# Hybrid block on one core: loads to the front, ten maximum steps into the loop, TensorE's order written out

## The chip, the cores and the metric

The kernel runs on one core of a Trainium2 chip. The metric is the device time of one execution in microseconds; the time before is the median of three runs. A profile of one further execution gives the duration of every instruction, what each engine waited for, and what the DMA queues moved.

## The reference

The kernel computes four residual stages over 2 x 2048 tokens of 256 features, all in 32-bit floats: a grouped-query attention, a feed-forward rotation, a linear attention and the feed-forward rotation again. Only the first stage is touched here:

```python
x = x + attn_a(layernorm(x))
# attn_a(x):                      B=2, N=2048, 16 query heads in 4 groups over 4 key heads, head size 16
q = x @ Wq + bq;  k = x @ Wk + bk;  v = x @ Wv + bv
scores = einsum('bghnd,bhsd->bghns', q, k)
attn   = softmax(scores / 4, axis=-1)        # over all 2048 keys of the batch
out    = einsum('bghns,bhsd->bghnd', attn, v)
return out @ Wo + bo
```

## The kernel before

**Blocks and units.** Tokens are handled in eight blocks of 512 (`NB = 8`; `BPB = 4` blocks make a batch). A unit is one block of queries with one of the four groups, so there are 32 units. For each unit the softmax needs the largest score of every query, and only then the exponentials. The kernel computes the scores twice. `largest()` makes them with queries on partitions (`s`, L378), and VectorE reduces each 128 x 512 tile to its maximum (`mx`, L382): 64 such maximum steps per unit. At the end of a unit `turn_maxima` transposes the negated maxima (`pm`, L398), ScalarE copies them (`mr`), and four DMAs on SP put them into `mrows` (`a_m`, L405). The main loop makes the scores again with keys on partitions (`p`, L633), adds the maxima with a second matmul (the shift, L637), takes the exponential on ScalarE (`e`, L641) and weighs the values (`av`, L620). It has 16 loop steps per unit, each with four scores, four shifts, four exponentials and four weighings. In each loop step four maximum steps of a later unit are mixed in with `next(ahead)`. So the maxima run ahead of the loop by a lead: `LEAD = 80` maximum steps are issued before the loop begins, that is the whole of unit 0 and sixteen of unit 1.

**The prologue** is everything before the loop. For block j, `arrive(j)` loads the tokens (`xs`, L255), `look(j)` computes mean and variance on VectorE and the scale on POOL, `spread(j)` normalizes into `z`, `features(j)` transposes on TensorE (`tr`) and copies out (`zb`), `keys(j)` multiplies by the key and value weights (`pk`), splits the keys into a high and a low half (`kh`, `kl`), stores the halves to DRAM (`dk`, L244) and fetches them in the layout that the scores need (`a_kP`, L249). `asked(j, m)` projects queries (`pq`, L337), `project(u)` stores and fetches a unit's queries (`dq`, `qP`), and `values(j)` transposes the values (`pv`). Blocks 0 to 3 are written out by hand; the rest is the generator `pieces()`, one piece after every third lead step. `biases` multiplies selection rows with the bias columns (`a_pbias`, `a_pbq`); their copies `bkv` and `bq` are used by `keys` and `asked`. `rows()` loads the output weights (`a_wo`, eight DMAs, and `a_bo`) and makes the output bias row.

**Queues and order.** SP issues its DMAs in order: one that waits for computed data holds those behind it. Before the change the loads of blocks 0 to 3 are at the front of SP's order, block 4 is behind the stores and fetches of block 1's keys (L543), and blocks 5 to 7, two constants and the output weights are behind unit 1's queries (L560 to L567). ACT's queue carries the weights at the start.

The framework may move instructions of an engine; `in_order` ties them to the program's order. Before the change, all five engines are tied at the loop's start, for what was issued up to there:

```python
            in_order(begin, (engines.PE, engines.DVE, engines.Activation, engines.Pool, engines.SP))
```

In the built program the first loop steps' scores on TensorE stand among the last lead steps: after the fourth score of the first loop step, for instance, four lead steps follow before its first shift. The maximum steps of unit 0 take their banks from two pools (`psp` with four, `pss` with three); later units use the three of `pss` alone. The loop's `p` tiles use the four of `psp`.

Of the kernel before, what the change touches and what calls it, by code (L numbers as in the profile page):

```python
# [16 lines left out]
P = 128  # L17
# [50 lines left out]
def tile_hybrid(ctx: ExitStack, tc: tile.TileContext, x: bass.AP, consts: bass.AP, wa_d: bass.AP, wf_d: bass.AP, wb_d: bass.AP, out: bass.AP):  # L68
# [84 lines left out]
    def attention_a():  # L153
        with ExitStack() as st:
# [41 lines left out]
            def biases(raw, at, bqr, sel):  # L196


                pb = psp.tile([P, BLK], F32, tag="p", name="a_pbias")
                rows, bv = sel[:, 0:64], sel[0:1, 64:P]  # L200
                compact(rows, ident, nc.scalar.copy)
                compact(bv, raw[0:1, at["bv"][0] : at["bv"][1]], nc.scalar.copy)
                mm(pb[0:64, 0:1], rows, raw[:, at["bk"][0] : at["bk"][1]], start=True, stop=True)
                mm(pb[64:P, 0:1], bv, ones[0:1, 0:1], start=True, stop=True)
                pq = psp.tile([P, BLK], F32, tag="p", name="a_pbq")
                for e in range(2):
                    mm(pq[64 * e : 64 * e + 64, 0:2], rows, bqr[:, e::2], start=True, stop=True)
                nc.vector.tensor_copy(bkv, pb[:, 0:1])
                nc.vector.tensor_copy(bq, pq[:, 0:2])
# [52 lines left out]
            def look(j):  # L262

                st = own.tile([P, 4, 6], F32, tag="ln_st", name=f"st_a{j}", bufs=4)
                mv = own.tile([P, 4, 2], F32, tag="ln_mv", name=f"mv_a{j}", bufs=4)
                rs, nb = (own.tile([P, 4], F32, tag=f"ln_{t}", name=f"{t}_a{j}", bufs=4) for t in ("rs", "nb"))
                for t in range(4):
                    if t == 3:
                        yield
                    nc.vector.bn_stats(st[:, t, :], xs[:, 4 * j + t, :])  # L270
                for t in range(4):
                    nc.vector.bn_aggr(mv[:, t, :], st[:, t, :])
                nc.vector.tensor_scalar(rs, mv[:, :, 1], EPS, None, ALU.add)
                nc.gpsimd.tensor_tensor(rs, rs, const("mhalf"), ALU.pow)
                nc.vector.tensor_scalar(nb, mv[:, :, 0], -1.0, None, ALU.mult)
                nc.gpsimd.tensor_tensor(nb, nb, rs, ALU.mult)
                looks[j] = mv, rs, nb
                yield

            normal, planes, kvs = {}, {}, {}  # L280

# [206 lines left out]
                        nc.vector.tensor_tensor(xs[:, 4 * j + t, :], xs[:, 4 * j + t, :], po[:, 0:D], ALU.add)  # L488
                        yield

            LEAD, WARM = 64 + 16, 4
            ahead = largest()
            begin = len(nc.cur_bb.bb.instructions)
            loads = ExitStack()
# [12 lines left out]
            arrive(1)  # L507
            nc.scalar.dma_start(wqb, wa_d[:, slice(*_WA["wq"])])
            nc.scalar.dma_start(bqr, wa_d[:, slice(*_WA["bq"])])
            arrive(2)  # L510
            arrive(3)

            nc.vector.memset(still, 0.0)
            idle = psp.tile([P, BLK], F32, tag="p", name="idle")
# [5 lines left out]
            for n, first in (("wk", 0), ("wv", 64)):  # L520
                for c in range(2):
                    lo = at[n][0] + c * P
                    compact(wkv[:, c, first : first + 64], raw[:, lo : lo + P], nc.scalar.copy)
            list(look(0))
            biases(raw, at, bqr, sel)
            one, two, three = look(1), look(2), look(3)
            next(one)
            spread(0, ld, 2)
            next(one)
            features(0, ld, 1)  # L530
            compact(wq.rearrange("p c d -> p (c d)"), wqb, nc.gpsimd.tensor_copy)
            spread(1, ld, 2)
            keys(0, ld)()
            features(1, ld, 0)
            list(two)
            asked(0, 0)
            first = project(0, nc.gpsimd)
            spread(2, ld, 2)
            list(three)
            first()  # L540
            second = keys(1, ld)
            second()
            arrive(BPB)  # L543
            values(0)
            features(2, ld, 1)
            spread(3, ld, 2)
# [10 lines left out]
            next(ahead)  # L557
            next(ahead)
            project(1)()
            nc.sync.dma_start(small[:, P : _CONST["ones"][0]], consts[:, P : _CONST["ones"][0]])  # L560
            nc.sync.dma_start(
                small[:, _CONST["ones"][1] : _CONST["mhalf"][0]], consts[:, _CONST["ones"][1] : _CONST["mhalf"][0]]
            )
            for j in range(BPB + 1, NB):
                arrive(j)
            more = rows()
            next(more)  # L567

            def memsets():
                for t in mrows[0] + mrows[1]:  # L570
                    nc.gpsimd.memset(t.bitcast(F32), 0.0)
# [4 lines left out]
            def pieces():  # L576

                memsets()
                list(look(4))
                values(3)  # L580
                for j in range(1, BPB):
                    for m in range(2):
                        asked(j, m)
                        yield
                        if (j, m) == (2, 0):
                            spread(4, ld, 0)
                next(more)
                for j in range(BPB, NB):
                    features(j, ld, 0)
                    if j + 1 < NB:  # L590
                        list(look(j + 1))
                    yield
                    keys(j, ld)()
                    if j + 1 < NB:
                        spread(j + 1, ld, 0)
                    yield
                    asked(j, 0)
                    yield
                    asked(j, 1)
                    values(j)  # L600
                    if j == BPB:
                        next(more)
                    yield

            rest = pieces()
            for n in range(4, LEAD):
                next(ahead)
                if n % 3 == 1:
                    next(rest, None)
                if n == 67:  # L610
                    for f in later:
                        f()
                    later.clear()
            in_order(begin, (engines.PE, engines.DVE, engines.Activation, engines.Pool, engines.SP))

            av, last, done, norms = None, None, iter(()), iter(())

# [5 lines left out]
                    )  # L623

            for u, kb in ((u, kb) for u in range(len(units)) for kb in range(KB)):
                qP, mrow = queries[u], mrows[u % 2]
                k0 = units[u][0] // BPB * N + kb * P
                t, es = [], []

                def score(r):  # L630
                    row = slice(64 * (r % 2), 64 * (r % 2) + 64)
                    t.append(psp.tile([P, BLK], F32, tag="p", name=f"p{u}_{kb}_{r}"))
                    mm(t[r], kP[r // 2][row, k0 : k0 + P], qP[r // 2][row, :], start=True, stop=False)  # L633

                def shift(r):
                    row = slice(64 * (r % 2), 64 * (r % 2) + 64)
                    mm(t[r], pick[row, :], mrow[r // 2][row, :], start=False, stop=True)  # L637

                def exp(r):
                    es.append(sb.tile([P, BLK], F32, tag="e", name=f"e{u}_{kb}_{r}", bufs=8))  # L640
                    nc.scalar.activation(es[r], t[r], AF.Exp, scale=1.0 / HD**0.5)  # L641

                ready = list(later)
                later.clear()

                next(ahead, None)
                next(ahead, None)
                score(0)
                score(1)
                shift(0)  # L650
                shift(1)
                exp(0)
                exp(1)
                if kb == 1:
                    next(done, None)
                score(2)
                next(ahead, None)
                score(3)
                shift(2)
                next(ahead, None)  # L660
                shift(3)
                exp(2)
                exp(3)
                for f in ready:
                    f()
                if last is not None:
                    if last[1] == 0:
                        av = pav.tile([P, BLK], F32, tag="av", name=f"av{last[0]}")
                    weigh(*last)
                    if last[1] == KB - 1:  # L670
                        done = finish(last[0], av)
                last = u, kb, es
                if kb > 1:
                    next(done, None)
                    next(norms, None)
                if u % G == 1 and kb == 1 and G < u < 4 * G:
                    norms = norm(u // G - 1)
                if kb == 4 and u + 2 < len(units):
                    project(u + 2)()
                if rest is not None and next(rest, "end") == "end":  # L680
                    rest = None
                    loads.close()
                    late = later_pools["late"] = ctx.enter_context(tc.tile_pool(name="late", bufs=1, side="right"))
                    for n, (name, of) in enumerate((("wf", wf_d), ("wb", wb_d))):
                        weights[name] = late.tile([P, of.shape[1]], F32, name=name)
                        nc.sync.dma_start(weights[name], of)
                    for name in ("w4", "b3"):
                        at = slice(*_WF[name])
                        nc.sync.dma_start(weights["wf"][64:P, at], wf_d[0:64, at])
# [804 lines left out]
```

## Time and profile before

| | us |
|---|---|
| median of three runs | 2184.47 |
| lowest, highest | 2184.06, 2188.18 |
| the profiled execution, its own time | 2182.7 |
| its span, first to last instruction | 2180.8 |
| first maximum (`s`) on TensorE | 28.83 |
| unit 0's maxima turned (`pm`) | 101.04 |
| first shift of the loop (L637) | 105.58 |
| weighing of the fourth loop step begins | 124.26 |

A row of the timeline gives the start, the duration, engine, line, operation, output and inputs, the shape and a count; in brackets stands the idle time of the engine just before, and what ended it. A row of the windows gives, for a stretch of time, its length and then the busy time of PE, PEld (weight loads), DVE (VectorE), ACT (ScalarE) and POOL (GpSimd), each with its count, then the granted share of TensorE's clock, the mean busy share of the DMA engines, and GB/s. A row of the groups gives the count, the busy time, the mean duration in ns, and the idle time before with what ended it.

### The profile page before, as it was taken

The numbers are of one execution on the slowest core, as the hardware profiler recorded it, in microseconds if no ns is written. First come the engines' busy times: TensorE is split into PE (matmuls) and PEld (weight loads), VectorE is DVE, ScalarE is ACT, GpSimd is POOL, SyncE is SP. The second block draws the span as 40 slices with busy tenths as digits, with TensorE's granted clock in tenths as the row PEclk, the third lists the DMA queues.
The fourth block names the chain that finished last, engine by engine and source line by source line (L and its number), as shares of the span: only waits on it lengthen the run. The fifth ranks groups of instructions, "written<-read, shape, count | busy, mean of one in ns | idle before, by whom it ended". The sixth has DMA issues, their size and how long they took to land.

```text
span 2180.8 us, 38972 instructions
## 1 busy us (share of the span) xinstructions
PE 2136.0 (98%) x14346; PEld 1028.5 (47%) x14346; DVE 1725.7 (79%) x3319; ACT 1434.0 (66%) x2780; POOL 348.6 (16%) x318
## 2 busy tenths in 40 slices
PE   8899999999999999999999999999999999999998
PEld 3344444444444444444444444444444567676434
DVE  6789998998999899899899899987144688886435
ACT  3367777777776777777677777777864445554442
POOL 3100000000001000000000000000145345541450
PEclk9999999999999999999999999999999999999999
DMA  6410110101101011010110101100100000000002
GB/s 184 135 58 14 41 36 16 46 12 45 36 16 45 10 48 36 16 39 17 48 35 17 36 19 48 36 16 7 51 1 1 1 1 2 1 2 1 1 0 78
DMA packets 53552, 68.21 MB, mean 31 GB/s; under 512 B 18800, under 2 KB 27888, under 8 KB 53104
## 3 DMA queue, kind: packets, MB, share of 16 engines
q1 hardware_dynamic: 52448, 64.26, 10.6%
q8 instruction: 113, 1.85, 0.3%
q10 hardware_dynamic: 720, 0.92, 0.1%
q14 instruction: 79, 0.65, 0.1%
q0 software_dynamic: 192, 0.52, 0.1%
HBM read 35.26 MB, written 25.69 MB: 28 GB/s over the span
## 4 chain that ended last, share of the span: by engine, by line
PE 86%; DVE 8%; DMA 2%; ACT 1%; SPq 1%; issue 1%; POOL 1%; DVEq 0%; ACTq 0%; POOLq 0%
PE av L620 21%; PE s L378 19%; PE p L633 10%; PE q1f L796 7%; PE p L637 7%; DVE mx L382 5%; PE q2f L806 4%; PE pe L1084 2%; PE po L487 2%; PE bpo L1110 1%; PE pv L954 1%; PE pw L954 1%; PE pq L945 1%; PE q3f L816 1%; PE pk L945 1%; DMA xs<-in_x 1%
## 5 line engine op out<-in xcount | busy, mean ns | idle before, releaser
L382 DVE TENSOR_REDUCE mx<-s 128x1 f32<-128x512 f32 x2048 | 1272.9, 683 | 118.1 <-PE s L378 116.4
L641 ACT ACTIVATE e<-p 128x512 f32<-128x512 f32 x2048 | 1060.7, 605 | 356.9 <-PE p L637 353.3
L378 PE MATMUL s<-a_kP,qP 64*128 64x512 f32 x2048 | 706.7, 470 | 19.5 <-DVE mx L382 17.4
L637 PE MATMUL p<-a_m,a_pick 64*128 64x512 f32 x2048 | 589.5, 416 | 0.0
L378 PEld LDWEIGHTS s<-a_kP,qP 64*128 64x128 f32 x2048 | 283.1, 184 | 578.9 <-DVE mx L382 549.8
L620 PE MATMUL av<-e,a_v 128*32 128x512 f32 x4096 | 550.2, 605 | 0.0
L633 PE MATMUL p<-qP,a_kP 64*128 64x512 f32 x2048 | 529.1, 394 | 2.3 <-ACT e L641 2.3
L633 PEld LDWEIGHTS p<-qP,a_kP 64*128 64x128 f32 x2048 | 286.4, 185 | 62.8 <-ACT e L641 26.9
L637 PEld LDWEIGHTS p<-a_m,a_pick 64*128 64x128 f32 x2048 | 283.9, 184 | 29.4
L481 POOL TENSOR_TENSOR oc<-oc,sums 128x512 f32<-128x512 f32 x16 | 20.8, 1299 | 1232.7 <-DMA sums<-dr 907.1
L796 PE MATMUL q1f<-zq,wf 128*128 128x512 f32 x384 | 175.5, 600 | 0.0
L620 PEld LDWEIGHTS av<-e,a_v 128*32 128x32 f32 x4096 | 81.4, 108 | 128.5 <-issue 119.8
L797 ACT ACTIVATE a1f<-q1f,wf 128x512 f32<-128x512 f32 x96 | 66.0, 688 | 99.6 <-PE q1f L796 96.2
L796 PEld LDWEIGHTS q1f<-zq,wf 128*128 128x128 f32 x384 | 70.6, 190 | 98.0 <-issue 86.3
L806 PE MATMUL q2f<-a1f,wf 128*128 128x512 f32 x192 | 89.6, 610 | 0.0
L1090 DVE TENSOR_TENSOR en<-pe,small 128x512 f32<-128x512 f32 x128 | 79.4, 683 | 12.7 <-PE pe L1084 12.6
L835 DVE TENSOR_SCALAR cf<-cf,f_beta,alphaf 128x512 f32<-128x512 f32 x32 | 33.6, 1050 | 53.7 <-ACT cf L834 53.6
L839 POOL TENSOR_TENSOR tf<-cf,zq 128x512 f32<-128x512 f32 x32 | 55.6, 1737 | 92.0 <-DVE cf L835 91.7
L808 ACT ACTIVATE a2f<-q2f,wf 128x512 f32<-128x512 f32 x48 | 32.7, 687 | 54.9 <-PE q2f L806 54.9
L841 POOL TENSOR_TENSOR zq<-zq,tf 128x512 f32<-128x512 f32 x32 | 56.8, 1775 | 3.1 <-DVE tf L838 0.7
L806 PEld LDWEIGHTS q2f<-a1f,wf 128*128 128x128 f32 x192 | 35.2, 193 | 45.3 <-issue 44.4
L840 DVE TENSOR_TENSOR zq<-zq,tf 128x512 f32<-128x512 f32 x32 | 22.2, 693 | 36.2 <-POOL tf L839 36.0
(207 smaller groups left out, 1674.0 us busy)
## 6 DMA issues: line engine op xcount, KB each, us to landing
qP<-dq SPq DMA_DIRECT2D x64, 256.0 KB
dq<-qh SPq DMA_DIRECT2D x62, 128.0 KB
dq<-ql SPq DMA_DIRECT2D x62, 128.0 KB
a_kP<-dk SPq DMA_DIRECT2D x16, 256.0 KB
oc<-avs SPq DMA_DIRECT2D x128, 32.0 KB
sums<-dr SPq DMA_DIRECT2D x128, 32.0 KB
out<-xs SPq DMA_DIRECT2D x16, 256.0 KB
xs<-in_x SPq DMA_DIRECT2D x7, 512.0 KB
```

What stands on the lines that cost most here:

```text
L378: mm(s, qP[r // 2][row, qi * P : (qi + 1) * P], kP[r // 2][row, k0 + kb * BLK : k0 + (kb + 1) * BLK], start=True, stop=True,)
L382: nc.vector.tensor_reduce(mx[:, qi, r : r + 1, kb], s, AX.X, ALU.max)
L620: mm(av[32 * r : 32 * r + 32, :], vA[:, units[u][0] // BPB * KB + kb, 32 * r : 32 * r + 32], es[r], start=(kb == 0), stop=(kb == KB - 1),)
L633: mm(t[r], kP[r // 2][row, k0 : k0 + P], qP[r // 2][row, :], start=True, stop=False)
L637: mm(t[r], pick[row, :], mrow[r // 2][row, :], start=False, stop=True)
L641: nc.scalar.activation(es[r], t[r], AF.Exp, scale=1.0 / HD**0.5)
L796: mm(q1, w1[:, c, m * P : (m + 1) * P], z[:, c, :], start=(c == 0), stop=(c == 1))
L797: nc.scalar.activation(a1[:, m, :], q1, AF.Gelu, bias=b1[:, m : m + 1])
L806: mm(q2, w2[:, c, :], a1[:, c, :], start=(c == 0), stop=(c == 1))
L839: nc.gpsimd.tensor_tensor(t1, cs, z[:, 0, :], ALU.mult)
L841: nc.gpsimd.tensor_tensor(z[:, 1, :], z[:, 1, :], t1, ALU.subtract)
L1090: nc.vector.tensor_tensor(self.ens[t][w], pes[w].rearrange("p (h n) -> p h n", h=4), const("triu").unsqueeze(1).to_broadcast([P, 4, P]), A ...
```

## The change

- SP's loads of blocks 4 to 7, the two constants and the output weights are issued with the first loads, ahead of every store.
- `look` is no longer a generator. `look(1)` is issued after block 0 is normalized and transposed; before, three quarters of its first part stood ahead of block 0's normalization. Both copies of block 0's transposes are on ACT (one was on VectorE).
- `biases` stops after its two selection copies. Its four products are issued after block 0's transposes.
- The lead is 70 maximum steps. Ten more are taken inside the loop, one in every second of the first twenty loop steps.
- The turning of unit 0's maxima is issued at n = 66, ahead of the last projection of block 7; before, at n = 67, behind it.
- Six warm-up products in place of four.
- TensorE is tied to the program's order from the prologue through the first four loop steps, the other four engines at the loop's start as before.

```diff
                 compact(bv, raw[0:1, at["bv"][0] : at["bv"][1]], nc.scalar.copy)
+                yield
                 mm(pb[0:64, 0:1], rows, raw[:, at["bk"][0] : at["bk"][1]], start=True, stop=True)
...
                 for t in range(4):
-                    if t == 3:
-                        yield
                     nc.vector.bn_stats(st[:, t, :], xs[:, 4 * j + t, :])
...
                 looks[j] = mv, rs, nb
-                yield
...
-            LEAD, WARM = 64 + 16, 4
+            LEAD, MORE, WARM = 64 + 6, 10, 6
...
-            arrive(2)
-            arrive(3)
+            for j in range(2, NB):
+                arrive(j)
+            nc.sync.dma_start(small[:, P : _CONST["ones"][0]], consts[:, P : _CONST["ones"][0]])
+            nc.sync.dma_start(
+                small[:, _CONST["ones"][1] : _CONST["mhalf"][0]], consts[:, _CONST["ones"][1] : _CONST["mhalf"][0]]
+            )
+            more = rows()
+            next(more)
...
-            list(look(0))
-            biases(raw, at, bqr, sel)
-            one, two, three = look(1), look(2), look(3)
-            next(one)
+            look(0)
+            picked = biases(raw, at, bqr, sel)
+            next(picked)
             spread(0, ld, 2)
-            next(one)
-            features(0, ld, 1)
+            features(0, ld, 0)
+            look(1)
+            next(picked, None)
             compact(wq.rearrange("p c d -> p (c d)"), wqb, nc.gpsimd.tensor_copy)
...
             second()
-            arrive(BPB)
             values(0)
...
             project(1)()
-            nc.sync.dma_start(small[:, P : _CONST["ones"][0]], consts[:, P : _CONST["ones"][0]])
...
-            for j in range(BPB + 1, NB):
-                arrive(j)
-            more = rows()
-            next(more)
...
             for n in range(4, LEAD):
                 next(ahead)
-                if n % 3 == 1:
-                    next(rest, None)
-                if n == 67:
+                if n == 66:
                     for f in later:
                         f()
                     later.clear()
-            in_order(begin, (engines.PE, engines.DVE, engines.Activation, engines.Pool, engines.SP))
+                if n % 3 == 1:
+                    next(rest, None)
+            in_order(begin, (engines.DVE, engines.Activation, engines.Pool, engines.SP))
...
             for u, kb in ((u, kb) for u in range(len(units)) for kb in range(KB)):
+                if (u, kb) == (0, 4):
+                    in_order(begin, (engines.PE,))
...
                     next(norms, None)
+                if kb % 2 == 1 and u * KB + kb < 2 * MORE:
+                    next(ahead)
```

More of the change, by code (lines that the diff above doesn't have):

```diff
@@ L534, in attention_a @@
             features(1, ld, 0)
-            list(two)
+            look(2)
             asked(0, 0)
@@ L538, in attention_a @@
             spread(2, ld, 2)
-            list(three)
+            look(3)
             first()
@@ L559, in attention_a @@
             project(1)()
[L560 to L563, printed above, removed]
-            for j in range(BPB + 1, NB):
-                arrive(j)
-            more = rows()
-            next(more)
             def memsets():
@@ L578, in pieces @@
                 memsets()
-                list(look(4))
+                look(4)
                 values(3)
@@ L590, in pieces @@
                     if j + 1 < NB:
-                        list(look(j + 1))
+                        look(j + 1)
                     yield
```

## The prediction

> **What bounds the kernel now.** I read the page first: which engine carries the span.
>
> ```profile
> PE 2136.0 (98%) x14346; PEld 1028.5 (47%) x14346; DVE 1725.7 (79%) x3319; ACT 1434.0 (66%) x2780; POOL 348.6 (16%) x318
> ```
>
> PE is called busy 98% of 2180.8 us, so little is left except where PE is seen idle. Everything that the change moves is issued before about 160 us. After some 560 matmuls (unit 1, step 4 of the loop) the two programs hold the same matmuls in the same order. DVE's last difference is in the same place, and POOL's order is the same throughout. So the question is the prologue, up to the first exponentials at 106 us, and the first twenty loop steps. Next come the waits of PE in the timeline, with the wait on DVE that stands behind each.
>
> ```profile
> 36.95 0.50 PE L378 MATMUL s<-a_kP,qP 64*128 64x512 f32 x2
> 41.16 0.49 PE L378 MATMUL s<-a_kP,qP 64*128 64x512 f32 x1 [3.71 <-DVE mx L382]
> 41.59 3.33 PE L337 MATMUL pq<-zb,a_wq 128*128 128x512 f32 x4
> 44.85 1.01 PE L378 MATMUL s<-a_kP,qP 64*128 64x512 f32 x3
> 45.79 1.98 PE L337 MATMUL pq<-zb,a_wq 128*128 128x512 f32 x4
> ...
> 61.63 0.49 PE L378 MATMUL s<-a_kP,qP 64*128 64x512 f32 x1 [4.01 <-DVE mx L382]
> 62.05 3.32 PE L337 MATMUL pq<-zb,a_wq 128*128 128x512 f32 x4
> ```
>
> ```profile
> 38.56 1.40 DVE L270 BATCH_NORM_STATS2 st_a<-xs 128x6 f32<-128x256 f32 x4 [4.28 <-DMA xs<-in_x]
> ...
> 59.03 1.08 DVE L270 BATCH_NORM_STATS2 st_a<-xs 128x6 f32<-128x256 f32 x3 [3.75 <-DMA xs<-in_x]
> ```
>
> PE names the reduction L382 as its releaser, but DVE itself stood still: `look(4)` and `look(5)` are ahead of the reductions in DVE's order and wait for token blocks. Those blocks come late because SP issues them behind stores that wait for computed keys:
>
> ```profile
> 32.12 0.80 SPq L249 DMA_DIRECT2D a_kP<-dk  x2
> 32.96 0.43 SPq L255 DMA_DIRECT2D xs<-in_x  x1
> ...
> 51.28 0.80 SPq L249 DMA_DIRECT2D qP<-dq  x2
> 52.12 0.43 SPq L560 DMA_DIRECT2D small<-in_const  x1
> 52.60 0.43 SPq L561 DMA_DIRECT2D small<-in_const  x1
> 53.07 1.53 SPq L255 DMA_DIRECT2D xs<-in_x  x3
> ```
>
> The first projection after each stall takes 3.33 and 3.32 us where 1.98 is usual. The windows say why (PEclk is the number after POOL):
>
> ```profile
> 42.10:45.40 3.30, 3.30 (x6) 1.18 (x5) 2.00 (x4) 0.44 (x1) 0.00 (x0) 0.50 0.73 204
> 62.60:65.90 3.30, 3.30 (x7) 1.16 (x5) 2.29 (x5) 0.00 (x0) 1.72 (x3) 0.50 0.43 90
> 103.50:106.90 3.40, 2.77 (x10) 1.22 (x10) 3.40 (x7) 0.90 (x2) 0.00 (x0) 1.00 0.28 60
> 107.00:110.30 3.30, 3.30 (x14) 2.49 (x12) 2.72 (x5) 2.25 (x5) 0.00 (x0) 0.50 1.02 426
> ```
>
> Last, the way into the loop. The first shift (L637, 105.58) waits for the turned maxima `pm`, their copy, and four DMAs that start at 102.28; meanwhile DVE works through twelve bare lead steps:
>
> ```profile
> 101.04 0.60 PE L398 MATMUL pm<-small,mt 128*8 128x128 f32 x4
> 102.10 7.35 DVE L382 TENSOR_REDUCE mx<-s 128x1 f32<-128x512 f32 x12 [2.06 <-PE s L378]
> 105.58 0.39 PE L637 MATMUL p<-a_m,a_pick 64*128 64x512 f32 x1
> ```
>
> One maximum step so costs DVE 7.35/12 = 0.61 us, and PE 0.22 (three between projections, 50.28 to 50.95).
>
> **The change, part by part.**
>
> *Loads first, up to the first maximum (28.83 us before).* SP now issues 21 DMAs before its first key store: 4.78 MB, with ACT's 0.92 MB 5.7 MB in all. The trace moved 316 GB/s from 2.5 to 12 us and 361 from 8 to 11.3, so the last load lands between 18.3 and 20.5. SP is held that long, since its issues wait for earlier landings (the eight `a_wo` issues of 0.3 to 0.45 us took 7.74 us behind three token loads). The first key stores go at about 20 instead of 16.78. From that store to the end of both `a_kP` fetches was 5.2 us, so `qP` is fetched at 25.2. It went at 26.31 before, held by `dq` (POOL's stores of the first queries, landed 26.17). `dq` itself comes 1 to 2 us earlier. The first scaling no longer stands behind `look(1)`'s wait for block 1 (9.80), and the biases' products, whose `bqr` landed at 9.0, stand behind the first transposes. Moving block 0's first copy to ACT adds about 0.5 us to that chain. From fetch to first maximum was 2.5 us: 27.7. Bounds: -2.5 (`dq` alone decides) and +2 (the loads at 250 GB/s); I take **-0.8**. Two more warm-up products are four passes of 0.43, ending near 8.4: they cost nothing, because PE's next work waits for block 0 until past 9.
>
> *The token stalls go.* 3.71 + 4.01 us, and the slow windows behind them: 1.35 + 0.28 and 1.34 + 0.30 on the projection and the three maxima. Together 11.0. What is late next? Two looks, 2.0 us of DVE each, ran inside the stalls and now fall among the reductions, where DVE has 0.7 us spare per piece (48.24, 50.82). `look(6)`, in that position already, holds PE for 0.81 (71.66), so I give back 0.8. POOL's 22.3 us wait for `a_bo` goes too, with nothing behind it that PE needed. Keys don't take over: SP's later fetches had finished at 32.9, 40.7 and 46.3 and now follow the first `qP` at 5.6 us each (about 31, 37 and 42), while their maxima start at about 42, 57 and 70. **-10.2.** The block-7 key product `pk7`, at 92.56, starts at 81.6.
>
> *Into the loop.* `pm` moves ahead of the last projection and values (2.4 us). But SP serves in order, and its last `a_kP` fetch ended at 100.87, 8.3 after `pk7`. It depends on `pk7`, ACT, DVE and POOL, not on `pm`. So `a_m` goes at `pk7` + 8.3, and the shift 3.3 later (102.28 to 105.58): +11.6 instead of +13.0. **-1.4**; the shift is at 93.2. PE, now strictly in order, has 9.4 us of work for those 11.6 and idles about 2.
>
> *Ten steps fewer in front.* From the first shift to the fourth step's weighing took 18.7 us before (105.58 to 124.26), with 24 reductions still to do. Now 20 remain: 12.3 us of DVE plus a start of 0.6; PE's own work is 11 us, or 12.7 with a slow window. I take 13.5: **-5.2**.
>
> *The ten steps come back.* Eight fall into the first unit after that point, two into the next unit. PE pays 8 x 0.22 = 1.7. DVE pays 4.9 but has only about 3.5 spare in a unit of 44 us:
>
> ```profile
> L382 DVE TENSOR_REDUCE mx<-s 128x1 f32<-128x512 f32 x65 | 40.4, 683 | 3.5 <-PE s L378 3.5
> ```
>
> Bounds 1.7 and 4.9; I take **+3.0**, as DVE becomes the slightly longer engine. With 70 + 4.5 per step, unit 1's `pm` comes one loop step later. It then has some 4.9 us before its use against 5.3 needed: **+0.5**.
>
> Sum: -0.8 - 10.2 - 1.4 - 5.2 + 3.0 + 0.5 = -14.1.
>
> *A rule to weigh.* The window 103.5 to 106.9 has PE busy by record, yet 107 to 110.3 ran at 0.50. The Trainium skill, "TensorE: Matmul & The Clock Gate", Part 1, says that the clock halves after a whole idle window of about 3.4 us. By that rule neither the 2 us hole before the first shift nor the one before the first maximum would cost anything, and the sum would be -15.7. The trace shows a window with ten matmul records followed by half clock, so gaps inside a window are enough; I keep the slow window (1.6) in step four, and put another for the first hole into the range.
>
> **The profiled execution** took 2182.7 us, span 2180.8: it would take 2168.6. It is 1.8 below the median of the runs, 2184.47; the same saving gives 2170.4, and I say 2170.
>
> **The rivals.**
>
> *DVE and PE get in each other's way (0.17).* With three `s` banks and strict order, each late reduction stops PE and then DVE. For: 149 weight loads waited on L382 between 112 and 320 us, and spare time is 8%. Against: those waits summed to only 1.7 us on the matmuls. If all 4.9 is paid in place of 3.0, some 2.7 more is lost to interlocking (0.14 in each of twenty steps), and the way to the fourth step saves 3.0 in place of 5.2, the gain is 14.1 - 1.9 - 2.7 - 2.2 = 7.3: 2177.
>
> *More is gained (0.09).* The first hole closes (`dq` decides, -2.5) and no slow window comes: -1.7 - 1.6 more, and DVE pays the minimum, -1.3: 2166.
>
> *The change doesn't reach the stall (0.04).* If something else were late at 38 and 59 (keys behind SP, a bank), the 11 us stay and only the last steps act: about 2181, no difference. Against: DVE's wait names the tokens both times.
>
> *Slower (0.04): the key stores starve behind the loads.* All later fetches are behind SP's 21 loads, so each us that the loads land late moves the whole prologue by one. Break-even is a first key store at 20 + 14 = 34 us, that is 5.7 MB at 180 GB/s; at 150 it would be about 2190. For: between 5.0 and 6.0 us, with small constants among the loads, the rate fell to 292 and 196 GB/s. Against: 361 GB/s was reached with the same token loads.
>
> **How the numbers follow.** The sum as it stands has 0.66, spread over 2165 to 2174. A measurement here can tell about 0.2%, 4.4 us, from no change. The sum and the first two rivals end below 2180.1. The third rival stands for no change, the last for slower. Faster 0.92, same 0.04, slower 0.04. The range 2163 to 2178 takes in both signs of the first step, the second slow window and the interlocking.
>
> **What would show it.** Right: no wait of DVE on `xs` after 15 us; L337 after the seventh lead piece at 1.98; first key store at 19 to 21 us; the first maximum at 27 to 29; `pm` at 85 to 88 with `a_m` held by the last `a_kP` fetch; the first shift at 92 to 95; DVE over 95% busy for one unit. Wrong: a first maximum after 31; PE waits of over 0.8 us on L382 in each of the twenty steps; a new wait of PE on a key fetch.

## The result and the profile after

The median is 2176.16 us (2175.66 to 2178.99, five runs) against 2184.47 for the kernel before on the same chip: a ratio of 0.9959, with a 95% interval of 0.9944 to 0.9973. So it is faster by 0.4%, or 8.3 us between the medians. The profiled execution took 2176.16 us, its span is 2174.3: 6.5 us less than the span before. All sums below are made between these two executions. The forecast was 2170, so the direction held, but a good half of the predicted 14 us arrived. Where the rest went is what the experiments had to find.

The page's first part, after. PE has four matmuls more (the two warm-up products) and the same busy time to a tenth, so the 6.5 us appear as less idle time. That they are the sum of larger gains and losses can't be read here.

```profile
PE 2136.0 (98%) x14350; PEld 1030.1 (47%) x14350; DVE 1723.5 (79%) x3318; ACT 1431.9 (66%) x2781; POOL 348.3 (16%) x318
```

PE's timeline, after, from the first maximum to the first shift (`s` is now L376, `pk` L308, `pq` L335, `pm` L396, the shift L634):

```profile
30.93 0.80 PE L376 MATMUL s<-a_kP,qP 64*128 64x512 f32 x2 [5.68 <-DMA qP<-dq]
31.66 3.78 PE L308 MATMUL pk<-zb,a_wkv 128*128 128x512 f32 x4
...
36.67 1.98 PE L335 MATMUL pq<-zb,a_wq 128*128 128x512 f32 x4
...
85.00 1.98 PE L308 MATMUL pk<-zb,a_wkv 128*128 128x512 f32 x4
...
90.15 0.60 PE L396 MATMUL pm<-small,mt 128*8 128x128 f32 x4
...
96.02 0.68 PE L634 MATMUL p<-a_m,a_pick 64*128 64x512 f32 x2 [0.92 <-DMA a_m<-mr]
```

From the first projection on, the two stalls of 3.7 and 4.0 us are gone and a projection takes 1.98 us. But PE stands for 5.68 us before the first maximum, which comes at 30.93 instead of 28.83, and the key product after it takes 3.78 us. DVE's looks (L269), after: none of these waits for tokens.

```profile
38.40 1.39 DVE L269 BATCH_NORM_STATS2 st_a<-xs 128x6 f32<-128x256 f32 x4
...
53.80 1.39 DVE L269 BATCH_NORM_STATS2 st_a<-xs 128x6 f32<-128x256 f32 x4
```

SP's issues, after. The eight output weights hold SP for 6.63 us. The first key store goes at 20.44, then the first key fetch and the first query fetch go directly one after the other:

```profile
13.23 6.63 SPq L216 DMA_DIRECT2D a_wo<-in_wa  x8
...
20.44 1.15 SPq L245 DMA_DIRECT2D dk<-kh  x2
...
25.55 0.83 SPq L250 DMA_DIRECT2D a_kP<-dk  x2
26.55 0.79 SPq L250 DMA_DIRECT2D qP<-dq  x2
...
92.51 0.80 SPq L250 DMA_DIRECT2D a_kP<-dk  x2
93.41 2.60 SPq L403 DMA_DIRECT2D a_m<-mr  x4
```

The windows, after, around the two holes and over the sixteen loop steps from the fourth to the twentieth weighing, and below it the same sixteen steps before. The clock is the number after POOL:

```profile
25.60:28.90 3.30, 0.00 (x0) 0.00 (x0) 0.05 (x1) 0.28 (x1) 1.21 (x1) 1.00 0.65 207
29.00:32.30 3.30, 1.37 (x3) 0.79 (x4) 0.54 (x1) 0.00 (x0) 0.00 (x0) 0.50 0.81 260
32.40:35.70 3.30, 3.30 (x8) 1.01 (x7) 0.65 (x2) 0.16 (x1) 0.00 (x0) 0.50 0.39 108
93.90:97.20 3.30, 2.07 (x12) 1.09 (x11) 2.39 (x5) 0.88 (x3) 0.00 (x0) 1.00 0.49 162
97.30:100.60 3.30, 3.30 (x13) 2.51 (x13) 2.59 (x5) 2.40 (x5) 0.00 (x0) 0.50 0.99 375
110.36:161.11 50.75, 50.53 (x335) 23.75 (x333) 45.40 (x78) 34.06 (x68) 3.62 (x2) 1.00 0.18 48
```

```profile
124.26:168.42 44.16, 43.94 (x326) 19.60 (x325) 40.60 (x70) 34.00 (x67) 3.62 (x2) 1.00 0.21 55
```

Two things to see. One empty window (25.6 to 28.9) is followed by two at half clock. The first of these two holds only 1.37 us of PE work and the second is full (3.30); after that the clock is whole again. And the sixteen loop steps take 50.75 us instead of 44.16, while DVE is busy for 45.40 of them (89%), so it isn't full.

The way from one program's time to the other's, with stages cut at the same instructions in both traces:

| stage | before | after | difference |
|---|---|---|---|
| start of the first lead projection (`pq` after block 3's key product, L337 / L335) | 32.48 | 36.67 | +4.2 |
| from there to the block-7 key product | 60.08 | 48.33 | -11.8 |
| from there to the first shift | 13.02 | 11.02 | -2.0 |
| first shift to the fourth weighing | 18.68 | 14.34 | -4.3 |
| fourth to twentieth weighing | 44.16 | 50.75 | +6.6 |
| all the rest | 2012.4 | 2013.2 | +0.8 |

The rest is the same work in both; in the kernels below it differs by some 5 us from one profiled execution to another. So the token stalls went as forecast and a little more; the start of the prologue and the ten steps inside the loop took back 10.8 us, where 2.7 were expected.

### The profile page after: what moved, and what is told of

It is laid out like the page before. It is cut to its first block, busy times and chain, and to the rows that moved or that the text cites. A ratio compares the mean times of both kernels' runs of the same rounds, so it can differ in the third digit from the quotient of the medians.

```text
span 2174.3 us, 38977 instructions
## 1 busy us (share of the span) xinstructions
PE 2136.0 (98%) x14350; PEld 1030.1 (47%) x14350; DVE 1723.5 (79%) x3318; ACT 1431.9 (66%) x2781; POOL 348.3 (16%) x318
## 4 chain that ended last, share of the span: by engine, by line
PE 88%; DVE 8%; ACT 1%; DMA 1%; issue 1%; POOL 1%; SPq 1%; DVEq 0%; ACTq 0%; POOLq 0%
PE av L615 21%; PE s L376 20%; PE p L630 10%; PE q1f L795 8%; PE p L634 6%; DVE mx L380 5%; PE q2f L805 4%; PE pe L1083 2%; PE po L485 2%; PE bpo L1109 1%; PE pv L953 1%; PE pw L953 1%; PE pq L335 1%; PE pq L944 1%; PE q3f L815 1%; PE pk L944 1%
## 5 line engine op out<-in xcount | busy, mean ns | idle before, releaser
L376 PE MATMUL s<-a_kP,qP 64*128 64x512 f32 x2048 | 706.3, 470 | 17.1 <-DVE mx L380 10.8
L634 PE MATMUL p<-a_m,a_pick 64*128 64x512 f32 x2048 | 593.0, 415 | 0.9 <-DMA a_m<-mr 0.9
L376 PEld LDWEIGHTS s<-a_kP,qP 64*128 64x128 f32 x2048 | 283.7, 184 | 574.7 <-DVE mx L380 541.3
L634 PEld LDWEIGHTS p<-a_m,a_pick 64*128 64x128 f32 x2048 | 285.6, 184 | 27.9 <-DMA a_m<-mr 1.7
```

What stands on the lines that cost most here:

```text
L376: mm(s, qP[r // 2][row, qi * P : (qi + 1) * P], kP[r // 2][row, k0 + kb * BLK : k0 + (kb + 1) * BLK], start=True, stop=True,)
```

## Experiments

The kernels below differ from the changed kernel unless it is said otherwise. They ran in three groups, each beside runs of the kernel before on the same chip (medians 2188.47, 2186.47 and 2187.95), so ratios to that are compared, not times. Times of single instructions come from each kernel's profile. "pk4" and "pk7" are the starts of the key products of blocks 4 and 7.

### Are the loads in front what delays the first maximum?

`late_loads`: the loads go behind the first key stores again, but those of the tokens further forward than before the change: block 4 ahead of block 1's stores and blocks 5 to 7 directly behind them. The two constants and the output weights are again behind unit 1's queries.

```diff
-            for j in range(2, NB):
-                arrive(j)
-            ...
-            next(more)
+            arrive(2)
+            arrive(3)
...
             first()
+            arrive(BPB)
             second = keys(1, ld)
             second()
+            for j in range(BPB + 1, NB):
+                arrive(j)
...
             project(1)()
+            nc.sync.dma_start(small[:, P : _CONST["ones"][0]], consts[:, P : _CONST["ones"][0]])
+            ...
+            next(more)
```

> The changed kernel with the loads of block 4 behind the first queries' fetch, of blocks 5 to 7 behind block 1's keys, and of the two constants and the output weights behind unit 1's queries. Theory one (the loads hold the first key stores, and the two fetches then queue back to back): first key store at 14 to 15 us instead of 20.4, the queries' fetch goes when POOL's stores have landed (23.3), first maximum at 25 to 26 instead of 30.9, no half clock at 29 to 36, and 6 to 8 us less than the changed kernel, near 2169. Rival: block 4 is late again and look(4) waits near 32 us, 3 to 4 us of it are given back, near 2172. Second rival: the hole before the first maximum is hidden later by another wait: no change.

Measured: ratio 0.9983 (0.9975 to 0.9992). The start did what was looked for: the first key store went at 14.36, the first maximum at 26.58, the key product behind it ran at 1.98, and pk4 was at 47.79, 6.0 us earlier than in the changed kernel. But pk7 was at 89.10, 4.1 later. The timeline of `late_loads` names a third thing, in neither theory:

```profile
61.42 0.75 POOL L221 TENSOR_TENSOR a_db<-small,a_bo 128x128 f32<-128x128 f32 x2 [24.59 <-DMA a_bo<-in_wa]
...
62.23 1.22 PE L226 MATMUL a_pb<-a_db,small 128*128 128x256 f32 x2 [6.47 <-POOL a_db L221]
```

The bias row `a_bo` is the last load in SP's order, POOL waits 24.6 us for it, and PE waits 6.5 us for POOL's product. From 59.5 to 69.7 the clock is then at one half. The prediction had said of this wait, as it stood in the kernel before, that nothing behind it was needed by PE; here PE has run out of other work at 55.8 and the load is issued at 59.49, where before it was issued at 62.43 and PE came to the product only at 68.56. `late_loads_2` mends just that: `a_bo` is issued with the first loads.

```diff
-                nc.sync.dma_start(bo, wa_d[:, slice(*_WA["bo"])])
...
             arrive(2)
             arrive(3)
+            nc.sync.dma_start(bo, wa_d[:, slice(*_WA["bo"])])
```

> As late_loads, but the small load of the output bias (a_bo, 1 KB) goes with the first loads; constants and output weights stay behind unit 1's queries. Theory one (the key stores were held by the loads, and late_loads lost its gain to the bias alone, whose row holds POOL, then PE for 6.5 us and the clock behind it): first maximum at 26 to 27, no wait at a_pb, block 7's key product at 79 to 80 instead of 85.0, 5 to 6 us less than the changed kernel, near 2170 where before is 2184. Rival (some other load is late in its place): less than 2 us gained.

Measured: ratio 0.9938 (0.9925 to 0.9951), span 2166.8. The gain at the start is now kept: pk7 at 79.42 against 85.00, the first shift at 90.15 against 96.02. SP and PE of `late_loads_2`:

```profile
14.28 1.16 SPq L244 DMA_DIRECT2D dk<-kh  x2
...
18.61 0.82 SPq L249 DMA_DIRECT2D a_kP<-dk  x2
23.76 0.80 SPq L249 DMA_DIRECT2D qP<-dq  x2
```

```profile
26.44 0.50 PE L375 MATMUL s<-a_kP,qP 64*128 64x512 f32 x2 [1.10 <-DMA qP<-dq]
26.88 1.98 PE L307 MATMUL pk<-zb,a_wkv 128*128 128x512 f32 x4
```

From the issue of the query fetch to the first maximum it takes 26.44 - 23.76 = 2.7 us here, and 30.93 - 26.55 = 4.4 in the changed kernel. What differs is the transfer directly before: here the key fetch was issued 5.2 us earlier, there only 1.0. `late_loads` shows the short time again (23.91 to 26.58), and the next kernel the long one.

`loads_only` is the kernel before with nothing but the loads brought to the front (of the diff of the change, the lines that move `arrive`, the two constants and `rows()`).

> The kernel before with one part of the change alone: all loads ahead of the first key store. Theory one (this part carries the whole gain, and the rest of the change cancels itself): no wait on tokens at 38 and 59 us, first maximum at 31 as in the changed kernel, then as before: about 7 us less than before, ratio near 0.997 to 0.996. Rival (the moved biases, the order into the loop and the ten steps bring something too): at most 4 us less than before.

Measured: ratio 0.9964 (0.9950 to 0.9977). The first maximum came at 34.39, not near 31. SP and PE of `loads_only`:

```profile
21.89 1.16 SPq L244 DMA_DIRECT2D dk<-kh  x2
...
28.93 0.83 SPq L249 DMA_DIRECT2D a_kP<-dk  x2
29.94 0.79 SPq L249 DMA_DIRECT2D qP<-dq  x2
```

```profile
34.39 0.79 PE L378 MATMUL s<-a_kP,qP 64*128 64x512 f32 x2 [5.52 <-DMA qP<-dq]
```

So the other edits at the start (biases, look, copies, warm-up) bring 34.39 - 30.93 = 3.5 us on top of the loads. The token stalls, though, go by the loads alone: from the first lead projection (40.12) to pk7 (88.44) it takes 48.32 us, as in the changed kernel (48.33; 60.08 before). This pk7 is 4.1 us earlier than before, of which only 1.4 are left at the twentieth weighing (167.00 against 168.42): between 101 and 111 us it ran at half clock for 10.2 us. Its interval overlaps the changed kernel's, so the times don't divide the gain between the loads and the rest of the change; the stages do.

### What does the first hole cost through the clock?

`fill_hole` puts twelve products on data that lies ready into the hole before the first maximum.

```diff
             third()
+            hot = psp.tile([P, BLK], F32, tag="p", name="hot")
+            for _ in range(12):
+                mm(hot, still[:, 0:P], still, start=True, stop=True)
             next(ahead)
```

> The changed kernel with twelve 128x512 products of no use before the first maximum, 5.2 us in a hole of 5.7. Theory one (the hole costs two slow windows behind it): no half clock between 29 and 36 us, block 3's key product at 1.98 instead of 3.78 us, the first projection of the pieces 2 us earlier, and 2 us less in all, near 2174. Rival (later waits hide it): no change. If the products end after the queries land, up to 1 us more.

Measured: ratio 0.9975 (0.9965 to 0.9985). I had counted one pass for each product; each is two passes of 0.43 us, so the twelve took 10.47 us and pushed the first maximum to 35.39. The clock did stay full (the key product takes 1.98), but the filler was longer than the hole. `fill_hole_6` has six products in the same place.

> As fill_hole, with six products in place of twelve (twelve took 10.5 us, since each is two passes of 0.43, and pushed the first maximum to 35.4). Theory one: they end near 30, the first maximum stays at 31, block 3's key product takes 1.98 us, and block 4's key product starts 2 us earlier than in the changed kernel (53.8). Rival: it stays at 53 to 54.

Measured, in one run: span 2175.3. PE of `fill_hole_6`:

```profile
25.02 5.32 PE L558 MATMUL hot<-still 128*128 128x512 f32 x12
31.04 0.50 PE L376 MATMUL s<-a_kP,qP 64*128 64x512 f32 x2 [0.70 <-DMA qP<-dq]
31.47 1.99 PE L308 MATMUL pk<-zb,a_wkv 128*128 128x512 f32 x4
```

The first maximum stands where it was (31.04 against 30.93), the key product takes 1.99 in place of 3.78, and pk4 comes at 51.82 instead of 53.81. So the two slow windows cost 2.0 us, shown by the profile. The whole run doesn't show them: its first shift is still 2.2 us earlier, but the rest of the span was 3 us longer in this execution, which is within what that rest varies by.

### What do the ten steps cost inside the loop?

`lead_80`: all of the change, but the lead of 80 as before, nothing extra in the loop.

```diff
-            LEAD, MORE, WARM = 64 + 6, 10, 6
+            LEAD, MORE, WARM = 64 + 16, 0, 6
```

> The changed kernel with a lead of 80 and no extra steps in the loop. Theory one (an extra step costs the loop 0.8 us, a bare one in the lead 0.43): the way from the first shift to the fourth weighing grows from 14.3 to 18 to 19 us, the next sixteen loop steps shrink from 50.8 to 44.2, together 2 to 3 us less, near 2173.5. Rival (the ten steps are cheaper in the loop, as the sum of the prediction had it): 2 us more, near 2178.

Measured: ratio 0.9937 (0.9924 to 0.9950). From `pm` to the fourth weighing it takes 23.47 us in place of 20.21 (+3.3), and from there to the twentieth 44.25 in place of 50.75 (-6.5). The number given for the way from the first shift was wrong, because the ten steps stand ahead of the shift, not behind it (101.25 against 96.02). The twentieth weighing starts at 158.20 in place of 161.11: taking ten steps into the loop saved 3.3 and cost 6.5.

Why 6.5, where DVE's spare time had been counted on? First, a loop step with a fifth maximum, from the timeline of the changed kernel:

```profile
131.99 1.07 PE L615 MATMUL av<-e,a_v 128*32 128x512 f32 x8
...
132.99 0.73 PE L376 MATMUL s<-a_kP,qP 64*128 64x512 f32 x3
...
133.52 3.08 DVE L380 TENSOR_REDUCE mx<-s 128x1 f32<-128x512 f32 x5 [0.45 <-PE s L376]
...
134.26 0.50 PE L376 MATMUL s<-a_kP,qP 64*128 64x512 f32 x1
...
134.86 0.50 PE L376 MATMUL s<-a_kP,qP 64*128 64x512 f32 x1
...
135.29 1.07 PE L615 MATMUL av<-e,a_v 128*32 128x512 f32 x8
```

Three maxima fill the three banks at once; the other two must wait for a reduction each (134.26, 134.86: 0.60 apart, one reduction). DVE's idle time falls around the weighings: before this step's first reduction it stood for 0.45. The step takes 135.29 - 131.99 = 3.30 us against the usual 2.70: one reduction more. So DVE's spare time lies in gaps between the steps, and three banks don't carry work across them. Over eight steps this is 8 x 0.60 = 4.8 us. That the number of banks is what stops it is read from these waits; no kernel here had a fourth. The groups of the changed kernel, for these sixteen steps, show that the gaps didn't fill: 5.2 us of idle time before the reductions, where the same sixteen steps had 3.4 before the change (the row with the prediction, 3.5, is of 143 to 187 us):

```profile
L380 DVE TENSOR_REDUCE mx<-s 128x1 f32<-128x512 f32 x73 | 45.2, 682 | 5.2 <-PE s L376 4.5 <-PE p L630 0.8
```

Second, eight of the sixteen steps take 0.23 more, also some without a fifth maximum (129.06 to 131.99 is 2.93). The next two kernels look for the reason.

`pairs`: the ten extra steps are taken two at a time, every fourth loop step.

```diff
-                if kb % 2 == 1 and u * KB + kb < 2 * MORE:
+                if kb % 4 == 3 and u * KB + kb < 2 * MORE:
+                    next(ahead)
                     next(ahead)
```

> The changed kernel with the ten extra steps taken as five pairs, two in every fourth loop step, so that the maxima always start a loop step on the two different row halves. Theory one (two maxima in a row on the same half of the rows don't overlap on TensorE): loop steps without an extra take 2.70 us throughout instead of 2.70 and 2.93 in turn, about 2 us less in all, near 2174. Rival (VectorE alone sets the 0.8 us of an extra step): the sixteen steps stay at 50 to 51 us, no change.

Measured: ratio 0.9956 (0.9944 to 0.9968), 50.43 us for the sixteen steps: no gain, as the rival had it. But the expectation that pairs keep the cheap order was wrong, so this time alone does not decide against the theory; the single steps tell more. After each pair the loop steps change over: 2.70, then 2.93, then 2.70 again, with 3.91 or 4.13 for the step of the pair. A pair moves the maxima by two places in their order, and which two places are cheap follows from the program: `largest()` takes the four heads in the order 0, 1, 3, 2, even heads lie on the lower 64 rows and odd ones on the upper 64, and by the theory two neighbouring 64-row matmuls overlap only when they lie on different halves. Started two places on, a loop step has more neighbours on the same half. `lead_82` puts every step into that place: lead 82, nothing extra in the loop.

```diff
-            LEAD, MORE, WARM = 64 + 6, 10, 6
+            LEAD, MORE, WARM = 64 + 18, 0, 6
```

> The changed kernel with a lead of 82 and no extra steps: the maxima then stand two places further in the order of row parts (0, 1, 3, 2) through the whole loop. Theory (which two 64-row matmuls are neighbours decides whether they overlap; a loop step with the maxima in places 2 and 3 takes 2.93 us, in places 0 and 1 2.70): every loop step takes 2.93 us, about 0.23 x 490 = 110 us more than with a lead of 80, near 2285. Rival (the 2.93 us steps came from VectorE's backlog after the extra steps): 1 us more than with a lead of 80, near 2175.

Measured, in one run: 2282.18 us, 5% longer and within 3 us of the theory's number; the rival's is 107 us away. One loop step of `lead_82`, and below it one of `lead_80`, on PE:

```profile
140.00 1.06 PE L615 MATMUL av<-e,a_v 128*32 128x512 f32 x8
...
141.79 0.39 PE L630 MATMUL p<-qP,a_kP 64*128 64x512 f32 x2
142.01 0.39 PE L376 MATMUL s<-a_kP,qP 64*128 64x512 f32 x1
142.25 0.39 PE L634 MATMUL p<-a_m,a_pick 64*128 64x512 f32 x1
142.27 0.50 PE L376 MATMUL s<-a_kP,qP 64*128 64x512 f32 x1
142.61 0.39 PE L634 MATMUL p<-a_m,a_pick 64*128 64x512 f32 x1
142.93 1.07 PE L615 MATMUL av<-e,a_v 128*32 128x512 f32 x8
```

```profile
124.80 1.06 PE L615 MATMUL av<-e,a_v 128*32 128x512 f32 x8
...
126.59 0.39 PE L630 MATMUL p<-qP,a_kP 64*128 64x512 f32 x1
126.60 0.39 PE L376 MATMUL s<-a_kP,qP 64*128 64x512 f32 x1
126.82 0.39 PE L634 MATMUL p<-a_m,a_pick 64*128 64x512 f32 x1
126.83 0.38 PE L630 MATMUL p<-qP,a_kP 64*128 64x512 f32 x1
127.07 0.49 PE L376 MATMUL s<-a_kP,qP 64*128 64x512 f32 x1
127.07 0.50 PE L634 MATMUL p<-a_m,a_pick 64*128 64x512 f32 x1
127.50 1.07 PE L615 MATMUL av<-e,a_v 128*32 128x512 f32 x8
```

The same matmuls: 142.93 - 140.00 = 2.93 us against 127.50 - 124.80 = 2.70. Compare the second halves. In `lead_80` all six start in three pairs (at 126.6, 126.8 and 127.07). In `lead_82` the two scores make one pair (141.79) and a shift and a maximum another (142.25, 142.27), but one maximum (142.01) and the last shift (142.61) start alone: four slots in place of three, and a slot is 0.23 us. Over some 490 such steps this is about 110 us, and the span is 107.8 longer. The leads of 76 and 80, multiples of four, have the cheap order; the changed kernel's lead of 70 with single extra steps walks through all four places, two of which are dear. Eight steps times 0.23 is the missing 1.8 us, and 4.8 + 1.8 is the 6.6 of the table.

### What is the strict order on PE worth?

`order_free`: PE is tied at the loop's start like the other engines, as before the change.

```diff
-            in_order(begin, (engines.DVE, engines.Activation, engines.Pool, engines.SP))
+            in_order(begin, (engines.PE, engines.DVE, engines.Activation, engines.Pool, engines.SP))
...
-                if (u, kb) == (0, 4):
-                    in_order(begin, (engines.PE,))
```

> The changed kernel with TensorE tied only up to the loop's start, as before the change; the ten steps stay in the loop. Theory one (strict order in the first four loop steps is worth little): the fourth weighing comes 19 to 22 us after the maxima are turned, where the changed kernel takes 20.2, and the total is within 2 us of the changed kernel. Rival (the order brought the 4 us between the first shift and the fourth weighing): 23 us from the turning to the fourth weighing as before, 3 us more in all.

Measured, in one run: 2182.65 us. The rival held. Though `pm` came 0.8 us earlier than in the changed kernel (89.39 against 90.15), the fourth weighing came 2.1 later (112.48 against 110.36). At the twentieth it is 2.2 later; the other 4.3 us of the longer span lie behind that, in the part that varies.

The way from pk7 to the fourth weighing, once in each kernel's profile, divides the gain there: 31.70 us before, 25.36 after; 28.63 in `lead_80` and 28.25 in `order_free`. So on top of the rest of the change the ten steps fewer bring 28.63 - 25.36 = 3.3 us, and the strict order 28.25 - 25.36 = 2.9. Together they are 6.2 of the 6.3 gained, so if the two simply add up, the earlier turning of the maxima brings next to nothing by itself; that was not run alone.

These shares hold to about 1.2 us. Each is of one execution, and the clock takes part: on this way the kernel before, the changed kernel and `order_free` have one slow window of 3.4 us, `lead_80` has two (98.3 to 105.1). `late_loads_2` and `pairs` have the changed kernel's lead of 70 and its order on PE, but no slow window there, and take 24.11 and 24.26 us where it takes 25.36.

### Put together

`best_80` has the loads of `late_loads_2` and the lead of 80; `best_76` has those loads and a lead of 76, the nearest multiple of four towards 70, with nothing extra in the loop.

```diff
-            LEAD, MORE, WARM = 64 + 6, 10, 6
+            LEAD, MORE, WARM = 64 + 12, 0, 6
```

> late_loads_2 with a lead of 80 and no extra steps in the loop. If both findings are independent: 7 to 8 us less than the changed kernel, ratio to before about 0.992. Rival (the bare lead steps only fill a wait that is gone now): as late_loads_2 or worse.

> best_80 with a lead of 76, no extra steps. It keeps the maxima in the same places of a loop step (76 and 80 are both multiples of four) and takes four bare steps of 0.6 us out of the lead, of which the wait for the turned maxima covers one or two; at the end one more loop step carries maxima, 0.9 us. Theory one: 1 us less than best_80, within what a measurement can tell. Rival: each unit's maxima are turned one loop step later and come too late at every unit: up to 0.5 us times 31 more.

Measured: `best_80` 0.9922 (0.9908 to 0.9936), `best_76` 0.9908 (0.9894 to 0.9921), against 0.9959 (0.9944 to 0.9973) for the changed kernel: both are faster than it and than the kernel before, and the two can't be told apart by these intervals. The twentieth weighing starts at 152.28 and 149.26, where it was 168.42 before and 161.11 after the change. In `best_76` the sixteen steps take 44.26 us, as in the kernel before. The rival, that unit 1's maxima then turn too late, did not show: its steps run at 2.70 us.

## Why the prediction was right in sign and too large in size

**Up to the first maximum: predicted -0.8, measured +2.1, and +4.2 with the slow clock behind it.** The key store at about 20 was right (20.44), and so was its cause: `late_loads` stores at 14.36. The step that failed here is "From fetch to first maximum was 2.5 us: 27.7". That 2.5 was measured with SP's previous fetch long landed. Here the query fetch goes 1.0 us behind the key fetch and takes 4.4; the store to the end of the key fetches was also longer (20.44 to 26.38, 5.9 in place of 5.2). The bound of +2 was thus just passed, and the later times named beforehand were missed as well: `pm` came at 90.15, not 85 to 88, and the shift at 96.02, not 92 to 95. The rule weighed there, from the Trainium skill ("TensorE: Matmul & The Clock Gate", Part 1), names one idle window as the condition. The first slow window fits it: the hole had grown to 5.68 us and holds an empty window (25.6 to 28.9). The slow window at 97.3 does not: the one before it has 2.07 us of work in twelve matmuls. That the half clock lasted for a second window, after one with 1.37 us of work, is what the trace adds. To put the first hole "into the range" instead of into the sum was worth 2.0 us.

**The token stalls: predicted -10.2, measured -11.8.** Right. `loads_only` shows the cause. The give-back of 0.8 for the displaced looks was too much: PE waits only 0.17 and 0.18 us on the reductions near the looks, and the wait of 0.81 at 71.66, which the sum had left in place, is gone as well.

**Into the loop: predicted -1.4, measured -2.0.** The chain was named rightly: the last key fetch ended at 93.31, 8.3 after pk7 (85.00), and `a_m` went at 93.41. From there to the shift it took 2.6 us, not 3.3. The shift is late (96.02, not 93.2) by less than what the start had lost against its forecast.

**Ten steps fewer in front: predicted -5.2, measured -4.3.** The expected slow window is there (97.3 to 100.6), but by chance as much as by forecast, since `late_loads_2` and `pairs` have none. With the step above the sum is 6.3 where 6.6 were predicted, but the shares were wrong: the prediction gave the ten steps 5.2 and the strict order nothing of its own (it only lets PE idle for 2 us there), and `lead_80` and `order_free` show 3.3 and 2.9.

**The ten steps come back: predicted +3.0 and +0.5, measured +6.6.** The largest miss beside the first. "DVE pays 4.9 but has only about 3.5 spare" credited the spare time, and it can't be used. What was measured is the upper bound's rate, 0.60 for each extra step, on all eight of the stretch (4.8 us). The other 1.8 us, the order of row halves, was not in the sum, in no rival and outside the bounds. The check "DVE over 95% busy" was wrong for the same reason: 89%. The late turning of unit 1's maxima (+0.5) did not show.

**The rivals.** "DVE and PE get in each other's way" gave 2177, near the 2176.2 measured, and its first term, that all 4.9 is paid, came true. That its total is near is luck: of the 2.2 us that it took off the saving before the fourth step only 0.9 came true, the other 1.8 us in the loop had a different cause, and the miss at the start, 5.0 us against the forecast, is not in it. The slower rival had its mechanism (key stores behind the loads), and it was active, far from its break-even of 34 us for the first store. `late_loads_2` shows what it cost: some 6 us at the first shift.

## What to carry to other kernels

A load should pass the wait that blocks it, not everything: bring it ahead of the stalled store that holds it, and look at which small load in the same move another engine is waiting for. Spare time that an engine shows as an average is not yet time that can be used: ask whether buffers can carry work across its gaps. With three banks each extra reduction was paid in full. Where two row halves of the array overlap, an extra step changes who is whose neighbour in every later step, so shift such streams only by whole rounds of their order.

## What the hardware showed that was not expected

- Two fetches of 512 KB issued 1.0 us apart: from the second issue to its use it took 4.4 us, and 2.7 with 5.2 us between them. That they share the bandwidth is the likely reason: from 27.0 to 31.0 us the changed kernel's DMA engines were 93% busy and moved 313 GB/s, at which both fetches together take 3.4 us. No kernel here doubled or halved a fetch to prove it.
- A product of 128x128 with 128x512 in 32 bits took two passes of 0.43 us at full clock (24 passes, 10.47 us, for the twelve of `fill_hole`).
- After the hole before the first maximum, half clock outlasted a window with 1.37 of 3.3 us of work and ended after a full one (3.30). What brings it is not settled here: a window with 2.07 us of work was followed by half clock in the changed kernel (93.9 to 97.2), one with 2.54 was not in `pairs` (95.3 to 98.7), and one with 2.77 was before the change (103.5 to 106.9).
- The same matmuls in a loop step took 2.70 or 2.93 us, by the order of their row halves: 5% of the whole kernel (107.8 us between `lead_80` and `lead_82`).
